# Pairwise bilinear products: two rows per partition, three large stores per row, three groups loaded ahead, later loads from the scalar queue

## The chip, the cores and the metric

One core of one Trainium2 chip. The metric is device microseconds of one execution, median of several. A single-core program's state is told from its own runs: fast when within 1.5% of the fastest of the same kernel. All runs compared here are fast; one experiment has a single timed run, whose state is unknown, and it is marked. A profile gives a span that is 1.7 to 2.7 us shorter than the time of the same execution.

## The reference

```python
# x: (4096, 32, 64) float32, W: (64, 64) float32
vid = jnp.einsum('bfd,de->bfe', x, W)
idx_i, idx_j = jnp.triu_indices(32, k=1)        # 496 pairs i < j
return x[:, idx_i, :] * vid[:, idx_j, :]        # (4096, 496, 64)
```

It reads 33.6 MB and writes 520.1 MB, so writing is the task.

## The kernel before

The batch is cut into 32 tiles of 128; I call the work of one tile a row, since each partition holds one batch row of it. TensorE transposes the row and multiplies it with W, ScalarE copies the results to `vid`, VectorE makes the 31 products (field i with all j > i), and SyncE stores them in nine pieces from six buffers. Loads share SyncE's queue with the stores.

```python
    CHUNK = 66
    AHEAD = 2
    xpool = ctx.enter_context(tc.tile_pool(name="x", bufs=AHEAD + 1))
    opool = ctx.enter_context(tc.tile_pool(name="out", bufs=6))
    def load(t):
        xt = xpool.tile([P, F, D], F32, tag="x", name=f"x_{t}")
        nc.sync.dma_start(out=xt, in_=x[t * P : (t + 1) * P])
        return xt
    # ... (weights, identity)
    for t in range(NT):
        if t + AHEAD < NT:
            loaded.append(load(t + AHEAD))
        xt = loaded[t]
        # ... (16 transposes, 31 matmuls, 8 copies: vid)
        for c, (fields, size) in enumerate(chunks):
            ot = opool.tile([P, CHUNK, D], F32, tag="o", name=f"o_{t}_{c}")
            # ... (one tensor_tensor per field)
            nc.sync.dma_start(
                out=out[t * P : (t + 1) * P, start : start + size, :],
                in_=ot[:, :size, :],
            )
            start += size
```

## Time and profile before

| | before |
|---|---|
| time, median of the first 3 runs | 1330.84 us (1329.06 to 1335.5) |
| span of the profile | 1326.4 us |
| DMA share and rate from 100 to 700 us | 1.01, 425 GB/s |
| VectorE busy | 1142.0 us, 86% |
| data packets per DMA engine | 2,560 |
| stores | 288, of 0.9 to 2.2 MB |

How to read it: with a DMA share of one nearly everywhere, ask two questions only. Where is the share under one? And how many nanoseconds does an engine need per byte while it is one? The prediction works both out, and shows the lines. A view that matters throughout is the table of stretches: each line gives a stretch, its length, the granted TensorE clock, the DMA share (the mean busy share of the 16 engines) and GB/s.

### The profile page before, as it was taken

The page shows a single profiled execution, that of the slowest core. Times are in us where ns is not written, and L with a number is a line of the kernel's source. Part 1 is how long each engine was busy: PE and PEld are TensorE (multiplying, and loading weights), DVE is VectorE, ACT ScalarE, POOL GpSimd, SP SyncE. Part 2 cuts the span into 40 slices and gives each one's busy share as a digit, 9 for nine tenths or more (in the row PEclk, how much of TensorE's full clock was granted, in tenths as well). Part 3 has the DMA queues.
Part 4 walks back from the last instruction along what each step waited for, and adds up shares of the span by engine and source line. Part 5 has one row for each costly group of instructions (what it writes and reads, how often), then busy time and mean ns, then how long its engine had stood idle before and what let it go on. Part 6 is the DMA issues. An engine that isn't in the chain of part 4 may idle for free.

```text
span 1326.4 us, 7305 instructions
## 1 busy us (share of the span) xinstructions
PE 255.1 (19%) x2496; PEld 242.2 (18%) x2496; DVE 1142.0 (86%) x992; ACT 139.4 (11%) x257; POOL 0.7 (0%) x6
## 2 busy tenths in 40 slices
PE   5012220133201222103321022220122211233000
PEld 5012220133201222103321022220122211233000
DVE  5999888888888888889888888888888888988893
ACT  3011101011000110101101011010111010110000
POOL 0000000000000000000000000000000000000000
PEclk9566665555656666555565566655666655655555
DMA  6999999999999999999999999999999999999996
GB/s 270 403 429 431 427 418 427 422 429 423 421 423 421 428 428 423 425 425 426 428 427 425 425 426 428 426 424 426 425 424 428 420 429 425 418 428 430 425 430 292
DMA packets 46277, 554.16 MB, mean 418 GB/s; under 512 B 5280, under 2 KB 5280, under 8 KB 9376
## 3 DMA queue, kind: packets, MB, share of 16 engines
q1 hardware_dynamic: 46080, 553.67, 98.9%
q8 instruction: 19, 0.31, 0.1%
q14 instruction: 18, 0.15, 0.0%
q10 hardware_dynamic: 160, 0.03, 0.0%
HBM read 33.59 MB, written 520.09 MB: 417 GB/s over the span
## 4 chain that ended last, share of the span: by engine, by line
DMA 75%; DVE 21%; issue 2%; PE 1%; DVEq 0%; ACT 0%
DMA out_dram<-o 75%; DVE o L117 21%; DMA x<-in_r_x_dram 0%; PE pv L97 0%; PE pt L85 0%; DVEq L117 0%; ACT vid L106 0%; DVEq L151 0%
## 5 line engine op out<-in xcount | busy, mean ns | idle before, releaser
L117 DVE TENSOR_TENSOR o<-x,vid 128x1984 f32<-128x1984 f32 (+30 forms) x992 | 1142.0, 1219 | 163.6 <-DMA out_dram<-o 149.1
L85 PE MATMUL pt<-ident,x 128*128 128x128 f32 x512 | 111.0, 406 | 967.9 <-DMA x<-in_r_x_dram 967.5
L85 PEld LDWEIGHTS pt<-ident,x 128*128 128x128 f32 x512 | 100.5, 219 | 971.9 <-issue 970.9
L86 ACT COPY xT<-pt 128x512 f32<-128x512 f32 x128 | 74.2, 589 | 702.2 <-PE pt L85 702.1
L97 PE MATMUL pv<-w,xT 64*128 64x64 f32 x1984 | 146.5, 308 | 0.0
L97 PEld LDWEIGHTS pv<-w,xT 64*128 64x128 f32 x1984 | 141.7, 222 | 8.7 <-issue 8.7
L106 ACT COPY vid<-pv 128x512 f32<-128x512 f32 (+1 forms) x128 | 64.2, 585 | 386.9 <-DVE o L117 382.6
L86 ACT ACT_TABLE_LOAD x1 | 1.3, 1283 | 2.0 <-issue 2.0
masks.py:199 POOL TENSOR_SCALAR_AFFINE_SELECT ident<-ident 128x128 f32<-128x128 f32 x1 | 0.3, 295 | 0.1
masks.py:197 POOL MEMSET ident<- 128x128 f32 x1 | 0.2, 205 | 0.3 <-POOLq L142 0.3
L142 POOL MEMSET const-bfloat16-1.0<- 128x1 bf16 x1 | 0.1, 102 | 0.0
L142 POOL MEMSET const-uint8-127<- 128x1 uint8 x1 | 0.1, 102 | 0.0
L142 POOL MEMSET const-float32-0.0<- 128x1 f32 x1 | 0.1, 99 | 0.2 <-issue 0.2
L142 POOL MEMSET const-float32-1.0<- 128x1 f32 x1 | 0.1, 99 | 0.0
## 6 DMA issues: line engine op xcount, KB each, us to landing
out_dram<-o SPq DMA_DIRECT2D x64, 1824.0 KB, 23.1
out_dram<-o SPq DMA_DIRECT2D x32, 2112.0 KB, 22.2
out_dram<-o SPq DMA_DIRECT2D x32, 2016.0 KB, 21.7
out_dram<-o SPq DMA_DIRECT2D x32, 1984.0 KB, 21.5
out_dram<-o SPq DMA_DIRECT2D x32, 1952.0 KB, 24.3
out_dram<-o SPq DMA_DIRECT2D x32, 1696.0 KB, 23.9
out_dram<-o SPq DMA_DIRECT2D x32, 1568.0 KB, 23.2
x<-in_r_x_dram SPq DMA_DIRECT2D x32, 1024.0 KB, 24.1
```

The source lines that it names most:

```text
L85: nc.tensor.transpose(pt[:, k, :], xt[:, f : f + 2, :], ident)
L86: nc.scalar.copy(xT[:, g * TPB : (g + 1) * TPB, :], pt)
L97: nc.tensor.matmul(pv[:, h, k, :], lhsT=xT[h * D : (h + 1) * D, pair, :], rhs=w2[h * D : (h + 1) * D, :], start=True, stop=True,)
L106: nc.scalar.copy(vid[:, g * GRP + k0 : (g + 1) * GRP, h, :], pv[:, h, k0:, :])
L117: nc.vector.tensor_tensor(ot[:, at : at + n, :], xt[:, i : i + 1, :].to_broadcast([P, n, D]), vid[:, i + 1 :, :], ALU.mult,)
L142: nc = _bacc.Bacc("TRN2", target_bir_lowering=False, num_devices=1)
```

## The change

The intent: fewer and longer packets, more work queued before the first store is ready, and loads that don't stand behind stores. The diff, cut to its core:

```diff
+SLOTS = [(0, 6), (6, 13), (13, 31)]
+FIRST = [(13, 31, [24, 18, 13]), (6, 13, [10, 8, 6]), (0, 6, [4, 2, 0])]
+SECOND = [(0, 6, [2, 4, 6]), (6, 13, [8, 10, 13]), (13, 31, [18, 31])]
-    AHEAD = 2
+    R = 2
+    G = B // (P * R)
+    SLOT = 171
+    AHEAD = 3
+    xg = x.rearrange("(g p r) f d -> g p r f d", p=P, r=R)
+    og = out.rearrange("(g p r) n d -> g p r n d", p=P, r=R)
-    opool = ctx.enter_context(tc.tile_pool(name="out", bufs=6))
+    opool = ctx.enter_context(tc.tile_pool(name="out", bufs=3))
+    def load(g):
+        queue = nc.sync if g < AHEAD else nc.scalar
+        xt = xpool.tile([P, R, F, D], F32, tag="x", name=f"x_{g}")
+        if g == 0:
+            h = F // 2
+            nc.sync.dma_start(out=xt[:, 0, h:, :], in_=xg[g][:, 0, h:, :])
+            nc.sync.dma_start(out=xt[:, 0, :h, :], in_=xg[g][:, 0, :h, :])
+            # ... (the second row as a third load)
+        else:
+            queue.dma_start(out=xt, in_=xg[g])
+    for g in range(G):
+        xt = loaded[g]
+        for r in range(R):
+            # ... (vid of this row, four fields at a time; row 0 from the last field down)
+            for s, (lo, hi) in enumerate(SLOTS):
+                # ... (rows 0 and 1 in the pieces of FIRST and SECOND, later rows whole)
+                ot = opool.tile([P, SLOT, D], F32, tag="o", name=f"o_{t}_{s}")
+                    nc.sync.dma_start(
+                        out=og[g][:, r, off[a] : off[b], :],
+                        in_=ot[:, off[a] - base : off[b] - base, :],
+                    )
+        if g + AHEAD < G:
+            loaded.append(load(g + AHEAD))
```

More of the change, by code (lines that the diff above doesn't have):

```diff
@@ L10 @@
 ALU = mybir.AluOpType
-def field_chunks(nf, most):
-    chunks, cur, size = [], [], 0
-    for i in range(nf - 1):
-        n = nf - 1 - i
-        if cur and size + n > most:
-            chunks.append((cur, size))
-            cur, size = [], 0
-        cur.append(i)
-        size += n
-    chunks.append((cur, size))
-    return chunks
+SLOTS = [(0, 6), (6, 13), (13, 31)]
+FIRST = [(13, 31, [24, 18, 13]), (6, 13, [10, 8, 6]), (0, 6, [4, 2, 0])]
+SECOND = [(0, 6, [2, 4, 6]), (6, 13, [8, 10, 13]), (13, 31, [18, 31])]
 @with_exitstack
@@ L37, in pairwise_bilinear_kernel @@
     B, F, D = x.shape
-    NT = B // P
+    NP = F * (F - 1) // 2
+    R = 2
+    G = B // (P * R)
     TPB = 4
-    GRP = 8
-    NGRP = F // (2 * GRP)
-    CHUNK = 66
-    AHEAD = 2
+    GRP = F // 2 // TPB
+    SLOT = 171
+    AHEAD = 3
+    xg = x.rearrange("(g p r) f d -> g p r f d", p=P, r=R)
+    og = out.rearrange("(g p r) n d -> g p r n d", p=P, r=R)
+    off = [i * (F - 1) - i * (i - 1) // 2 for i in range(F)]
     const = ctx.enter_context(tc.tile_pool(name="const", bufs=1))
-    xpool = ctx.enter_context(tc.tile_pool(name="x", bufs=AHEAD + 1))
-    tpool = ctx.enter_context(tc.tile_pool(name="xT", bufs=2))
+    xpool = ctx.enter_context(tc.tile_pool(name="x", bufs=AHEAD))
+    tpool = ctx.enter_context(tc.tile_pool(name="xT", bufs=1))
     vpool = ctx.enter_context(tc.tile_pool(name="vid", bufs=2))
-    opool = ctx.enter_context(tc.tile_pool(name="out", bufs=6))
+    opool = ctx.enter_context(tc.tile_pool(name="out", bufs=3))
     ps_t = ctx.enter_context(
-        tc.tile_pool(name="ps_t", bufs=3, space=bass.MemoryType.PSUM)
+        tc.tile_pool(name="ps_t", bufs=4, space=bass.MemoryType.PSUM)
     )
@@ L57, in pairwise_bilinear_kernel @@
     )
-    def load(t):
-        xt = xpool.tile([P, F, D], F32, tag="x", name=f"x_{t}")
-        nc.sync.dma_start(out=xt, in_=x[t * P : (t + 1) * P])
-        return xt
-    loaded = [load(t) for t in range(min(AHEAD, NT))]
     w2 = const.tile([P, D], F32)
@@ L69, in pairwise_bilinear_kernel, with project @@
     nc.scalar.dma_start(out=w2[D : 2 * D, :], in_=w)
+    def load(g):
[5 more added lines that the diff above has]
+            nc.sync.dma_start(out=xt[:, 0, :h, :], in_=xg[g][:, 0, :h, :])
+            for r in range(1, R):
+                nc.sync.dma_start(out=xt[:, r], in_=xg[g][:, r])
+        else:
+            queue.dma_start(out=xt, in_=xg[g])
+        return xt
+    loaded = [load(g) for g in range(AHEAD)]
     ident = const.tile([P, P], F32)
     make_identity(nc, ident)
-    chunks = field_chunks(F, CHUNK)
-    for t in range(NT):
-        if t + AHEAD < NT:
-            loaded.append(load(t + AHEAD))
-        xt = loaded[t]
-        xT = tpool.tile([P, F // 2, P], F32, tag="xT", name=f"xT_{t}")
-        for g in range(F // 2 // TPB):
-            pt = ps_t.tile([P, TPB, P], F32, tag="pt", name=f"pt_{t}_{g}")
-            for k in range(TPB):
-                f = 2 * (g * TPB + k)
-                nc.tensor.transpose(pt[:, k, :], xt[:, f : f + 2, :], ident)
-            nc.scalar.copy(xT[:, g * TPB : (g + 1) * TPB, :], pt)
-        vid = vpool.tile([P, F // 2, 2, D], F32, tag="vid", name=f"vid_{t}")
-        for g in range(NGRP):
-            pv = ps_v.tile([P, 2, GRP, D], F32, tag="pv", name=f"pv_{t}_{g}")
-            for k in range(GRP):
-                pair = g * GRP + k
+    def project(xt, r, tag, order):
+        xT = tpool.tile([P, F // 2, P], F32, tag="xT", name=f"xT_{tag}")
+        vid = vpool.tile([P, F // 2, 2, D], F32, tag="vid", name=f"vid_{tag}")
+        for g in order:
+            pairs = range(g * TPB, (g + 1) * TPB)
+            pt = ps_t.tile([P, TPB, P], F32, tag="pt", name=f"pt_{tag}_{g}")
+            for k, pair in enumerate(pairs):
+                nc.tensor.transpose(
+                    pt[:, k, :], xt[:, r, 2 * pair : 2 * pair + 2, :], ident
+                )
+            nc.scalar.copy(xT[:, g * TPB : (g + 1) * TPB, :], pt)
+            pv = ps_v.tile([P, 2, 2 * TPB, D], F32, tag="pv", name=f"pv_{tag}_{g}")
+            for k, pair in enumerate(pairs):
                 for h in range(2):
-                    if pair == 0 and h == 0:
-                        continue
                     nc.tensor.matmul(
@@ L103, in pairwise_bilinear_kernel @@
                     )
-            for h in range(2):
-                k0 = 1 if g == 0 and h == 0 else 0
-                nc.scalar.copy(
-                    vid[:, g * GRP + k0 : (g + 1) * GRP, h, :], pv[:, h, k0:, :]
-                )
-        vid = vid.rearrange("p g h e -> p (g h) e")
-        start = 0
-        for c, (fields, size) in enumerate(chunks):
-            ot = opool.tile([P, CHUNK, D], F32, tag="o", name=f"o_{t}_{c}")
-            at = 0
-            for i in fields:
-                n = F - 1 - i
-                nc.vector.tensor_tensor(
-                    ot[:, at : at + n, :],
-                    xt[:, i : i + 1, :].to_broadcast([P, n, D]),
-                    vid[:, i + 1 :, :],
-                    ALU.mult,
-                )
-                at += n
-            nc.sync.dma_start(
-                out=out[t * P : (t + 1) * P, start : start + size, :],
-                in_=ot[:, :size, :],
-            )
-            start += size
+            nc.scalar.copy(
+                vid[:, g * TPB : (g + 1) * TPB].rearrange("p k h e -> p h k e"),
+                pv[:, :, :TPB, :],
+            )
@@ new lines, in project, with products @@
+        return vid.rearrange("p g h e -> p (g h) e")
+    def products(xt, vid, ot, base, r, fields):
+        for i in fields:
+            n = F - 1 - i
+            nc.vector.tensor_tensor(
+                ot[:, off[i] - base : off[i] - base + n, :],
+                xt[:, r, i : i + 1, :].to_broadcast([P, n, D]),
+                vid[:, i + 1 :, :],
+                ALU.mult,
+            )
+    for g in range(G):
+        xt = loaded[g]
+        for r in range(R):
+            t = g * R + r
+            first = t == 0
+            vid = project(xt, r, t, range(GRP - 1, -1, -1) if first else range(GRP))
+            plan = FIRST if first else SECOND if t == 1 else None
+            for s, (lo, hi) in enumerate(SLOTS):
+                if plan:
+                    lo, hi, ends = plan[s]
+                else:
+                    ends = [hi]
+                ot = opool.tile([P, SLOT, D], F32, tag="o", name=f"o_{t}_{s}")
+                base = off[lo]
+                at = hi if first else lo
+                for e in ends:
+                    a, b = (e, at) if first else (at, e)
+                    products(xt, vid, ot, base, r, range(b - 1, a - 1, -1) if first else range(a, b))
+                    nc.sync.dma_start(
+                        out=og[g][:, r, off[a] : off[b], :],
+                        in_=ot[:, off[a] - base : off[b] - base, :],
+                    )
+                    at = e
+        if g + AHEAD < G:
+            loaded.append(load(g + AHEAD))
```

## The prediction

> **What bounds the kernel now.** I began with the page's slices and its DMA packets line, since a kernel that writes 520 MB is likely held by its transfers.
>
> ```profile
> DVE  5999888888888888889888888888888888988893
> DMA  6999999999999999999999999999999999999996
> GB/s 270 403 429 431 427 418 427 422 429 423 421 423 421 428 428 423 425 425 426 428 427 425 425 426 428 426 424 426 425 424 428 420 429 425 418 428 430 425 430 292
> DMA packets 46277, 554.16 MB, mean 418 GB/s; under 512 B 5280, under 2 KB 5280, under 8 KB 9376
> HBM read 33.59 MB, written 520.09 MB: 417 GB/s over the span
> ```
>
> The DMA engines are full in 38 of 40 slices at about 425 GB/s; only the first and last slices are low. VectorE is at eight or nine tenths, so it is next in line, but not the bound. The waits say the same.
>
> ```profile
> DVE o L117 <- DMA out_dram<-o: 149.1, 172, 2.3
> DVE o L117 <- ACT vid L106: 14.5, 1, 14.5
> ...
> SPq L124 <- DVE o L117: 1151.0, 288, 16.7
> SPq L151 <- DMA out_dram<-o: 19.3, 1, 19.3
> ```
>
> VectorE waits 149 us for stores to free its output buffers. The last store takes 19.3 us to land after everything else. SyncE's long wait is only an issuer waiting for its next job. Then the stretches, to see where the DMA engines are not full (the columns after each stretch's length are the granted TensorE clock, the DMA share and GB/s).
>
> ```profile
> 2.00:9.50 7.50, 1.00 0.95 395
> 9.50:19.50 10.00, 1.00 0.04 16
> 19.50:100.00 80.50, 0.59 1.01 417
> 100.00:700.00 600.00, 0.56 1.01 425
> 700.00:1312.00 612.00, 0.56 1.01 426
> 1312.00:1326.40 14.40, 0.50 0.28 119
> ```
>
> Two holes. From 9.5 to 19.5 us nothing moves: three loads are done, and the first store is issued only at 18.8 us, after transposes, matmuls, copies and two products. From 1312 us only some of the 16 engines still work. Between the holes a faster compute engine buys nothing; only fewer nanoseconds per byte would.
>
> **A model of the transfers.** The trace's packet records, grouped by size, give medians of 272 ns (7,168 B), 309 (8,192), 469 (12,544) and 629 (16,896). They lie on a line: 0.03677 ns per byte plus 8.4 ns per packet. Each engine also writes a 4-byte completion packet (9 ns) per transfer. One engine moves a sixteenth of 553.65 MB, 34.603 MB, in 2,560 data packets (32 loads and 288 stores of 8 each) and 320 completions: 1272.2 + 21.5 + 2.9 = 1296.6 us. To test it I subtracted this cumulative sum from the 16 landings of each transfer. The earliest landing of each keeps a constant distance (within 0.2 us) from about the 12th transfer to the 230th, nearly 1,000 us: the fastest engine runs exactly at the model with no idle time. The latest landing falls behind it by 0.4 us at first, 3 us after 160 us, 12 us after 550 and 14 or 15 from 900 on. The steps come mostly at the x loads (about 0.2 to 1 us each), and some at the 16 KB instruction fetches. So the span is 1296.6 + about 14 of start (latency plus hole) + 15 of the slowest engine's lag + 0.7 of end = 1326.3, against 1326.4 measured. The tail is this lag, not the size of the last store.
>
> [...]
>
> **The change, part by part.**
>
> *Packets.* Stores: three per row instead of nine, the first two rows in 9 and 8 pieces: 30 x 3 + 17 = 107 transfers. Loads: 15 of 16 KB per partition, plus group 0 in three pieces: 18. Each gives an engine 8 packets, 1,000 instead of 2,560, and 125 completions instead of 320. The store packets are 39 and 44 KB. If each stays one packet: 1272.2 + 8.4 + 1.1 = 1281.7 us, a gain of 14.9. It counts in full, for the engines have no idle time to hide it in.
>
> *Start.* Three groups, 6.3 MB, are now ahead of the stores: 14.8 us of transfers instead of 7.4, so they last to about 17 us. (No bytes are added; only moved into the hole.) Meanwhile group 0's first half row should land near 4.4 us, the weights near 6.7 as before. Eight matmuls (1 us at the present 3.9 for 31) and one copy (0.6) put the first product at about 8.5. Seven short products, by their means of 218 to 618 ns less overlap, take 2.5 us: first store issued at about 11, of 0.9 MB. The next follow near 16, 22 and 26 us with 2.1, 2.6 and 2.0 MB. At 425 GB/s the work queued reaches to 19, 24, 30 and 35 us, always past the next issue. The hole closes. What is left is latency: the first load now lands at 5.6 us, 2.5 of it data, so about 3.2. Gain about 10.9.
>
> *Three output buffers of 5.6 MB instead of six of 2.1.* When the slowest engine lands a store, VectorE needs 11 to 13 us to refill that buffer (sums of the product means), plus some 2 to start the store; the other two buffers hold 25 us of work. So the slowest engine never starves, though the fastest may be held once it is over about 10 us ahead. The slowest sets the end, so this costs nothing. VectorE does the same 992 products: 35.7 us per row against 40 of transfers.
>
> *TensorE, ScalarE.* 64 more matmuls and regrouped copies, on engines 19 and 11 per cent busy: nothing. A scalar queue that blocks on a load waits for the same product that frees its next vid buffer, a row ahead: nothing.
>
> *The lag.* Thirteen loads run amid stores instead of 29, each twice the bytes. In the bursts before, the first four or five packets of a load on an engine nearly all took 309 ns, and slow ones (400 to 1,400) came later. That suggests that [...]reading in bursts is what costs. Dealt between 1.6 us stores, this should be milder. I choose 10 us for the lag and fetches, instead of 15: an estimate.
>
> *Sum.* 1281.7 + 3.2 + 10 + 0.7 = 1295.6 us of span. The times before are 4.4 above the profile's span (1330.84 against 1326.4). So 1300 us, 2.3% less: 14.9 from packets, 10.9 from the start, 5 from the lag.
>
> **The rivals.** (a) *Long packets are split*, say in two: 2,000 packets, only half the packet gain, 1308 us. For it: nothing over 16,896 B is in the trace. Against: 7 to 17 KB are all single packets on one line. (b) *Interleaved reads stall.* The 16 KB instruction fetches, dealt between stores, took 880 to 970 ns where the line says 611. If each of the 104 load packets per engine lost 0.3 us, 31 us would eat the gain: about 1320 to 1325. Against: [...]8 KB fetches took 309. (c) *The tail of 14 us stays or grows* because only three buffers bind the engines: 1305. (d) *Only the holes counted* and the steady rate stays 425 GB/s because HBM sets it: 1319. Against: the constant distance of the fastest engine[...]. (e) *Better*: the lag nearly vanishes with the burst reads, 1293. (f) *VectorE becomes the bound* for want of buffers: its idle share falls from 12%, but 12 us of slack per buffer speak against it.
>
> **Range and chances.** The line for two per cent is 1304.2 us (1330.84 x 0.98), only 4 above my number: (a), (b), (c) and (d) end above it; the main sum and (e) below. I give 1288 to 1318 eight times in ten; faster by over 2% 0.62, within 2% 0.35, slower 0.03.
>
> **What would show it.** Right: about 18,000 packets, store packets of about 1,617 ns (44 KB), a rate of 429 to 431 GB/s in the middle, no gap between 9.5 and 19.5 us, first store near 11 us, VectorE's waits for stores shorter in number and longer each, and a last stretch with a low DMA share of 10 us or less. Wrong: twice the store packets (a); load packets near 900 ns and a middle rate at or under 425 (b, d); an equally long tail (c); stretches in the middle with a DMA share clearly under 1, with VectorE full (f).

## The result, and the profile after

1301.91 us, median of four runs (1301.52 to 1302.08), against 1330.28 of the kernel before in the same rounds (1329.06 to 1335.5). The ratio is 0.9762, 95% interval 0.9728 to 0.9795. (A ratio is the mean of one kernel's fast runs over the mean of the other's in the same rounds, so not quite the ratio of the medians.) The span is 1300.3 us, 26.1 less. The medians differ by 28.4: the profiled run of the kernel before was one of its faster ones (1326.4, where its runs of later rounds have spans of 1325.7 to 1335.9).

The page of the changed kernel, the lines that answer to those in the prediction:

```profile
DVE  6999979889798897988979899798987979999991
DMA  9999999999999999999999999999999999999997
GB/s 384 430 421 439 428 430 436 423 432 430 428 429 430 434 422 436 435 422 433 433 429 431 423 434 424 430 435 428 433 426 427 437 421 430 434 433 431 436 431 318
DMA packets 18193, 554.12 MB, mean 426 GB/s; under 512 B 2160, under 2 KB 2160, under 8 KB 2544
```

The first slice is full now; the last is still low. The 18,193 packets, 46,277 before, are what one packet per partition and transfer gives, with the completions: the 44 KB packets were not split. The stretches of the changed kernel:

```profile
2.00:9.50 7.50, 1.00 0.99 378
9.50:19.50 10.00, 1.00 0.98 399
19.50:100.00 80.50, 0.61 1.02 430
100.00:700.00 600.00, 0.53 1.00 430
700.00:1200.00 500.00, 0.53 1.00 429
...
1285.90:1300.30 14.40, 0.50 0.39 170
```

Read each against its line of before. The 10 us hole, 16 GB/s then, moves 399 GB/s. The middle went from 425 to 430, with the same full share: more bytes per busy nanosecond. The last 14.4 us hold 0.39 instead of 0.28 of the engines, so the tail has changed little. The waits:

```profile
DVE o L112 <- DMA out_dram<-o: 130.2, 71, 4.7
...
DVE o L112 <- ACT vid L103: 11.1, 1, 11.1
```

VectorE still waits for stores, less often and longer each time (71 times up to 4.7 us, instead of 172 times up to 2.3). It remains ahead of the DMA engines. The issues on SyncE's queue, with start and length of the stretch in which they were issued:

```profile
2.11 1.34 SPq L72 DMA_DIRECT2D x<-in_r_x_dram  x2
13.61 44.99 SPq L137 DMA_DIRECT2D out_dram<-o  x12
```

The first store leaves at 13.61 us; before, at 18.80. I had said 11. It did no harm: the DMA share is 0.98 over the whole former hole, since 6.3 MB of loads are queued in front.

**The time split up.** I use the line of the prediction (0.03677 ns per byte, unrounded 0.036765, 8.4 ns per packet, 9 ns per completion) for each kernel's own packets. "Start" is 100 us less the time that the bytes of the first 100 us would have taken at the kernel's own middle rate (from 100 to 1200 us). Both are counted from the packet records, with a packet that runs across a boundary shared out by its time. (The table of stretches books it wholly where it starts; with packets of 1.6 us that would make the start of the changed kernel 1.3 us too small and its rest as much too large.) "Rest" is what remains of the span; most of it is how far the last of the 16 engines fell behind.

| kernel | span | line | start | rest |
|---|---|---|---|---|
| before | 1326.4 | 1296.6 | 13.6 | 16.2 |
| after | 1300.3 | 1281.7 | 4.8 | 13.8 |
| difference | 26.1 | 14.9 | 8.8 | 2.4 |

The line rests on packet durations, and those held: in the changed kernel the 7,680 packets of 43,776 B have a median of 1,618 ns (the line says 1,618) and the 3,840 of 39,424 B one of 1,458 (line 1,458). The table is of one run of each kernel; to which term the other 2.3 us between the medians belong, it can't say. Whether these shares are causes is for the experiments.

### The profile page after: what moved, and what is told of

Read it like the earlier page. It is cut to its first block, busy times and chain, and to the rows that moved or that the text cites. A ratio compares the mean times of both kernels' runs of the same rounds, so it can differ in the third digit from the quotient of the medians.

```text
span 1300.3 us, 6845 instructions
## 1 busy us (share of the span) xinstructions
PE 336.3 (26%) x2560; PEld 315.8 (24%) x2560; DVE 1132.8 (87%) x992; ACT 136.4 (10%) x257; POOL 0.7 (0%) x6
## 2 busy tenths in 40 slices
DMA packets 18193, 554.12 MB, mean 426 GB/s; under 512 B 2160, under 2 KB 2160, under 8 KB 2544
## 3 DMA queue, kind: packets, MB, share of 16 engines
q1 hardware_dynamic: 16128, 526.39, 94.5%
## 4 chain that ended last, share of the span: by engine, by line
DMA 62%; DVE 35%; issue 1%; PE 0%; DVEq 0%; ACT 0%
DMA out_dram<-o 61%; DVE o L112 35%; DMA x<-in_r_x_dram 0%; PE pt L88 0%; PE pv L96 0%; DVEq L166 0%; DVEq L112 0%; ACT vid L103 0%
## 5 line engine op out<-in xcount | busy, mean ns | idle before, releaser
L112 DVE TENSOR_TENSOR o<-x,vid 128x64 f32<-128x64 f32 (+30 forms) x992 | 1132.8, 1219 | 141.3 <-DMA out_dram<-o 130.2
L96 PE MATMUL pv<-w,xT 64*128 64x64 f32 x2048 | 230.0, 413 | 862.0 <-ACT vid L103 827.8
L96 PEld LDWEIGHTS pv<-w,xT 64*128 64x128 f32 x2048 | 218.2, 320 | 878.6 <-ACT vid L103 837.7
L103 ACT COPY vid<-pv 128x512 f32<-128x512 f32 x128 | 72.1, 587 | 1060.2 <-DVE o L112 971.3
L88 PEld LDWEIGHTS pt<-ident,x 128*128 128x128 f32 x512 | 97.6, 212 | 9.0 <-issue 5.3
L91 ACT COPY xT<-pt 128x512 f32<-128x512 f32 x128 | 66.4, 610 | 5.7 <-PE pt L88 5.6
## 6 DMA issues: line engine op xcount, KB each, us to landing
out_dram<-o SPq DMA_DIRECT2D x30, 4928.0 KB, 28.4
x<-in_r_x_dram SPq DMA_DIRECT2D x2, 2048.0 KB, 14.4
```

Source lines behind the costliest of these rows:

```text
L88: nc.tensor.transpose(pt[:, k, :], xt[:, r, 2 * pair : 2 * pair + 2, :], ident)
L91: nc.scalar.copy(xT[:, g * TPB : (g + 1) * TPB, :], pt)
L96: nc.tensor.matmul(pv[:, h, k, :], lhsT=xT[h * D : (h + 1) * D, pair, :], rhs=w2[h * D : (h + 1) * D, :], start=True, stop=True,)
L103: nc.scalar.copy(vid[:, g * TPB : (g + 1) * TPB].rearrange("p k h e -> p h k e"), pv[:, :, :TPB, :],)
L112: nc.vector.tensor_tensor(ot[:, off[i] - base : off[i] - base + n, :], xt[:, r, i : i + 1, :].to_broadcast([P, n, D]), vid[:, i + 1 :, :], ...
```

## The experiments

Each is one edit to the kernel before or to the changed one. All give correct results except the two without later loads, which are wrong on purpose. All numbers of "rest" and "start" are worked out as above. The kernel before ran beside each of them; its runs scatter by 0.8 per cent (1327.5 to 1337.7 us), those of the changed kernel by 0.04% in its own rounds. The changed kernel did not run again beside its variants. A span is that of one run too, so a difference of two or three us from the kernel before is within its scatter.

### More loads ahead, alone

```diff
-    AHEAD = 2
+    AHEAD = 6
```

> The kernel before with six loads ahead of the first store instead of two or three; nothing else. Theory of the start: 6.3 MB of loads last to about 17 us, the first store still comes at 18.8, so the hole of 10 us shrinks to about 3: 1323 us, about 7 less, and the rate in the middle stays 425 GB/s. Rival (the hole is free, since those loads were hidden later anyway): 1330.

Measured: 1320.42 us (1316.28 to 1325.32), ratio to before 0.9919 (0.9895 to 0.9942); span 1319.1. Its stretches:

```profile
9.50:19.50 10.00, 1.00 1.01 422
19.50:100.00 80.50, 0.64 0.97 404
```

The first of the next stretches alone, and the issue of the first store:

```profile
19.50:25.00 5.50, 1.00 0.53 220
22.04 0.35 SPq L124 DMA_DIRECT2D out_dram<-o  x1
```

The hole has moved and shrunk to 2.6 us (what is missing from a full share in those 5.5 us). I had forgotten that the loop issues one more load before the first row's work, seven in all; they fill the time up to 19.5 us. But the first store leaves at 22.04 us instead of 18.80: the 31 matmuls of the first row (62 records) took 7.09 us while the loads ran beside them, 3.99 before, when nothing moved. Start falls from 13.6 to 7.0, rest (15.5) and middle rate (425 GB/s) stay. The gain is 7.3 us by the spans and 10.6 by the medians: the hole was on the path.

### Three stores per row, alone

```diff
-    opool = ctx.enter_context(tc.tile_pool(name="out", bufs=6))
+    opool = ctx.enter_context(tc.tile_pool(name="out", bufs=3))
+    slots = [range(0, 6), range(6, 13), range(13, 31)]
-        for c, (fields, size) in enumerate(chunks):
-            ot = opool.tile([P, CHUNK, D], F32, tag="o", name=f"o_{t}_{c}")
+        for c, fields in enumerate(slots):
+            ot = opool.tile([P, 171, D], F32, tag="o", name=f"o_{t}_{c}")
 # and the store after the last field of a slot; in row 0 also at the old piece ends
```

> The kernel before with three large stores per row from three 5.6 MB buffers from row 1 on (row 0 in ten pieces, so that the start is as before); loads, their queue and one row per partition as before. Theory of packets: 1,080 data packets and 135 completions per engine instead of 2,560 and 320, so 14 us less: 1316 us, middle rate 430 GB/s, hole at the start unchanged. Rival (HBM sets the rate): 1330 and 425 GB/s. Rival (three buffers starve the engines): over 1330.

Measured: 1315.31 us (1314.45 to 1316.23), ratio 0.9881 (0.986 to 0.9902); span 1312.7.

```profile
9.50:19.50 10.00, 1.00 0.12 48
19.50:100.00 80.50, 0.58 0.99 414
100.00:700.00 600.00, 0.57 1.00 430
700.00:1200.00 500.00, 0.55 1.00 431
```

The hole is as before, and the middle has the changed kernel's rate with loads in the old queue and one row per partition. The span fell by 13.7 (the medians by 15.7), the line said 14.1; start (14.8) and rest (15.4) are near those of before. The higher rate comes from fewer packets or from the larger buffers, which changed with them; the next run takes the two apart.

### Nine stores per row put back

```diff
+                cuts = {0: [2, 4, 6], 6: [8, 10, 13], 13: [17, 21, 31]}[lo]
-                    nc.sync.dma_start(
-                        out=og[g][:, r, off[a] : off[b], :],
-                        in_=ot[:, off[a] - base : off[b] - base, :],
-                    )
+                    for c in [e] if plan else cuts:
+                        # one store of fields at..c, from the same buffer
```

> The changed kernel with each large store issued as three at the same moment from the same buffer: 287 stores instead of 107. Buffers, loads, start and queues unchanged. Theory of packets: 2,440 data packets and 305 completions per engine instead of 1,000 and 125, 13.7 us more: 1315 to 1316 us, middle rate 425 GB/s. Rival (larger buffers or the second queue raised the rate): 1302.

Measured: 1310.34 us (1309.91 to 1310.74), ratio to before 0.9843 (0.9822 to 0.9863); span 1309.0.

```profile
19.50:100.00 80.50, 0.64 1.01 426
100.00:700.00 600.00, 0.53 1.01 426
700.00:1270.00 570.00, 0.53 1.01 426
```

The rate is back at 426 with the same buffers, queues and start, so those three don't make it: fewer packets do. (By the line of packet durations it is the packets and not the size of a transfer: stores of 0.9 to 2.2 MB ran at 425 GB/s, of 5.0 to 5.6 MB at 430. No run changed the one without the other.) But the time rose by only 8.4 of the 13.7 us expected (the span by 8.7). The line explains the rate; what is missing is 1.0 in the start (3.8 instead of 4.8) and 4.0 in the rest (9.8 instead of 13.8). The tail is shorter with small stores: in the last 15 us the DMA share is 0.98, 0.94 and 0.19 per 5 us, and the 16 engines' landings of the last store are 6.0 us apart instead of 10.4. So in this kernel long packets win 13.7 us and give 4 back at the end. In the kernel before they gave nothing back (rest 16.2, then 15.4). Only with short stores do the dealt-in loads bring the rest to about what the prediction put down for lag and end, 10.7; why long stores beside them keep it up, no run shows.

### The old start in the changed kernel

```diff
-    AHEAD = 3
+    AHEAD = 2
-            h = F // 2
+            h = 0                       # group 0's first row in one load
 # ... (the load of the second half is taken out)
-            vid = project(xt, r, t, range(GRP - 1, -1, -1) if first else range(GRP))
-            plan = FIRST if first else SECOND if t == 1 else None
+            vid = project(xt, r, t, range(GRP))
+            plan = SECOND if t <= 1 else None
 # ... (and the products of row 0 in forward order)
```

> The changed kernel with the start of before: row 0 loaded whole and worked in forward order, and two groups (4.2 MB) ahead instead of three. Theory of the start: loads end near 12 us, the first store is issued near 19, so a hole of 8 to 9 us comes back: 1310 to 1311 us, middle rate unchanged at 430 GB/s. Rival (the start is free): 1302.

Measured: 1312.13 us (1309.66 to 1314.28), ratio 0.9856 (0.9833 to 0.9879); span 1307.7.

```profile
9.50:19.50 10.00, 1.00 0.29 121
19.50:100.00 80.50, 0.57 1.00 419
```

A hole comes back, and 7.4 us of span (10.2 of the medians). Start rises from 4.8 to 12.0, the middle stays at 430. From both sides the start is worth 7 to 11 us. More loads ahead did most of it in the kernel before; how the new order of the first row and the third group share it here, this run does not say, for it undoes both.

### Later loads on the sync queue

```diff
-        queue = nc.sync if g < AHEAD else nc.scalar
+        queue = nc.sync
```

> The changed kernel with the later loads issued from the sync queue, behind the stores, as before. Theory ([...]only the order of packets changes): the same number of packets, middle rate 430 GB/s; loads come in bursts again, so the lag of the slowest engine is 10 to 14 us as in the run with three stores added to the kernel before: 1302 to 1306 us. Rival (the second queue is a source of the gain): 1310 or more and a lower middle rate.

Measured: 1303.4 us (1303.07 to 1303.62), ratio 0.9775 (0.9755 to 0.9795); span 1301.5, middle rate 431 GB/s. From the changed kernel's page, its loads and their us to landing (last column):

```profile
x<-in_r_x_dram ACTq DMA_DIRECT2D x13, 2048.0 KB, 23.0
```

And from this run's:

```profile
x<-in_r_x_dram SPq DMA_DIRECT2D x15, 2048.0 KB, 29.6
```

On the scalar queue a load lands in 23 us, behind the stores in 29.6; nobody was waiting for it two groups ahead (TensorE waits for the first load only, 5 us in both). The order of the packets does change: of the 1,664 later load packets 1,443 start just as a store's packet ends, on the sync queue 8, where 1,425 follow another load packet. But the two times differ by only 1.5 us of 1302, in different rounds, and the intervals of the ratios overlap almost wholly: a gain from the move is not shown. By queue the packets took 94.5% and 4.9% of the 16 engines' time in the changed kernel, and 99.2% on the sync queue alone here: about the same in all.

### One row per partition

```diff
-    R = 2
+    R = 1
-    AHEAD = 3
+    AHEAD = 6
```

> The changed kernel with one row per partition and six groups of 1 MB ahead, so the same bytes are loaded ahead and the stores are the same. Theory (packets alone): 16 more loads, 128 more packets per engine, 1.2 us more: 1303. The load packets dealt between the stores are 8 KB instead of 16 KB, so the lag may change by some us either way. Rival (two rows per partition matter for themselves, by the longer run in memory): 1310 or more and a lower middle rate.

Measured: 1300.77 us (1300.28 to 1302.06), ratio 0.9757 (0.9736 to 0.9777); span 1299.0, middle rate 430 to 431. Two rows per partition did nothing that shows; the line's 1.2 us are within what the rest varies by (11.8 here).

### Two output buffers

```diff
-    opool = ctx.enter_context(tc.tile_pool(name="out", bufs=3))
+    opool = ctx.enter_context(tc.tile_pool(name="out", bufs=2))
```

> The changed kernel with two output buffers instead of three. Theory of slack (11 to 13 us to refill, about 2 to start a store, against 13 us of work in the one other buffer): the engines now run dry between stores, so the DMA share in the middle falls clearly under 1 and the time rises to between 1340 and 1400. Rival (buffers have no part in it, VectorE at 87 per cent is ahead anyway): 1302.

Measured: 1406.52 us, one run, state unknown; span 1404.7.

```profile
100.00:700.00 600.00, 0.52 0.92 391
700.00:1200.00 500.00, 0.53 0.92 394
```

The DMA share falls to 0.92, and the time is a little above my range. One run is enough for 8 per cent. So the third buffer carries the change, and the slack reckoned for it in the prediction is real: with one other buffer, 13 us of work don't cover the 11 to 13 us of refill and the start of the store. With two buffers no engine could run ahead either: the 16 landings of the last store came within 0.2 us of each other (10.4 in the changed kernel).

### Where the lag of the slowest engine comes from

The prediction put the lag before down to loads, chose 10 us for the changed kernel, and expected dealt-in loads to be milder. So I took the loads away, in both kernels. First the changed one:

```diff
-            loaded.append(load(g + AHEAD))
+            loaded.append(loaded[g])
```

> The changed kernel without the thirteen later loads (the first three groups are used again; the result is wrong on purpose). Bytes and packets taken away are worth 63.6 us per engine by the line of 0.03677 ns per byte and 8.4 ns per packet. Theory (loads amid stores make the slowest engine lag): the last stretch shrinks to about 3 us, so 7 us more are gained: about 1231 us. Rival (the lag comes from instruction fetches[...]): lag still about 10 us, 1238.

Measured: 1237.42 us (1237.38 to 1237.47); span 1235.6. This is the rival's number, 1238: the theory falls for the changed kernel. (The cause that the rival names isn't shown by it.) The landings of the last store are still 10.4 us apart, with 15 engines within the first 1.8 us and one alone at the end. That one engine falls back by 0.4 us in most rows, nearly always at the middle store: about 100 of the 3,840 packets of 39,424 B take 50 to 80 ns over the line, several in sequence 1.5 us apart, as on one engine. Then the kernel before:

```diff
-            loaded.append(load(t + AHEAD))
+            loaded.append(load(t + AHEAD) if t == 0 else loaded[t - 1])
```

> The kernel before without the 29 later loads (the first three are used again; wrong result on purpose). Bytes and packets taken away: 72.1 us by the line. Theory (in the kernel before the lag of 12 us comes from the loads, where its steps were seen): the lag falls to about 3 us, so 81 us less: 1250. Rival (lag without loads too, as in the changed kernel): 1259.

Measured: 1249.0 us (1248.79 to 1249.3); span 1246.5. Here the theory holds: the last store's landings are 4.1 us apart instead of 12.2, and the rest falls from 16.2 to 9.9. The share in the run's last stretches shows a short tail:

```profile
1236.00:1241.00 5.00, 0.50 0.94 397
1241.00:1246.50 5.50, 0.50 0.21 90
```

So the loads made the lag in the kernel before, and in the changed kernel something at the middle store makes one just as large without them. As the end is set by the slowest single engine, two such causes on different engines need not add up, and taking one away may show little; that is my explanation, no run takes both away. Three more runs asked what the middle store has. First the place of the buffers in SBUF:

```diff
+    opool = ctx.enter_context(tc.tile_pool(name="out", bufs=3))
     const = ctx.enter_context(tc.tile_pool(name="const", bufs=1))
 # ... and removed further down
```

> The changed kernel with the output buffers allocated first, so that they lie elsewhere in SBUF; nothing else. In the run without later loads one engine still fell behind by 0.4 us per row, always at the middle store, and about 100 of its 3,840 packets of 39,424 B took 50 to 80 ns too long. Theory (it is the place of the second buffer in SBUF): those packets go, the lag shrinks from 10 to between 5 and 8 us: 1297 to 1300 us. Rival (it is the packet's size or its place in HBM, or what else runs at that moment): the group stays with the 39,424 B packets, 1302.

Measured: 1301.35 us (1300.72 to 1302.06), ratio 0.9767 (0.9742 to 0.9791). Theory wrong: the group stays (77 packets at 60 to 80 ns over the line, among those of 39,424 B; 7 among those of 43,776 B). Next, which buffer a slot gets:

```diff
+    spare = opool.tile([P, SLOT, D], F32, tag="o", name="o_spare")
+    nc.gpsimd.memset(spare[:, 0, 0:1], 0.0)
     for g in range(G):
```

> The changed kernel with one unused output tile taken first, so that the three slots of a row go to the second, third and first buffer. Theory (place of the second buffer): the group of about 100 packets that take 50 to 80 ns too long moves from the 39,424 B packets to the 43,776 B ones; time within 2 us of 1302. Rival (size, HBM place or moment): it stays with the 39,424 B packets.

Measured: 1301.17 us (1300.16 to 1303.02), ratio 0.9767 (0.9741 to 0.9793). Wrong again: 75 of the 39,424 B packets, 14 of the others. Last, the size:

```diff
-SLOTS = [(0, 6), (6, 13), (13, 31)]
+SLOTS = [(0, 6), (6, 14), (14, 31)]
-    SLOT = 171
+    SLOT = 172
```

> The changed kernel with the boundary between the second and third slot moved by one field: from row 2 on the middle store is 44,032 B per partition and the last 39,168 B, with the same number of packets. Theory (the slow group of packets belongs to the middle store's place in the row or to its moment): a group of about 100 packets 50 to 80 ns over the line appears among the 44,032 B packets, and the lag and the time stay: 1300 to 1303 us. Rival (it belongs to packets of about 39 KB): the group appears among the 39,168 B packets. Third possibility (it belongs to just this size or start): the group is gone, the lag falls and the time is 1294 to 1298.

Measured: 1302.3 us (1300.98 to 1303.65), ratio 0.9779 (0.9755 to 0.9802). The group has moved to the 44,032 B packets of the middle store (60 at 60 to 80 ns over the line, 5 among those of 39,168 B). So it is not the buffer, its place or the packet's size, but the middle store's place in the output row or what else happens at that moment. The kernel before with three stores has the same middle store and hardly any such packets (2 of 3,968 between 50 and 300 ns over), so its place in the row alone can't be the whole cause either.

The kept traces show what happens at that moment: TensorE works on a later row. In the run without later loads, TensorE is busy for the whole of the time of the packets 50 to 80 ns over the line, and for 0.29 of the time of the middle store's packets on the line. In the changed kernel the two shares are 0.95 and 0.37. It is the same where such packets lie in other stores: 0.78 against 0.21 among those of 43,776 B in the kernel before with three stores, 1.00 against 0.22 among those of 14,592 B in the kernel before. And the steps of 0.4 us end with the middle store that lands at 1136 us; TensorE's last matmul ends at 1138. The 20 instruction fetches, about 0.3 us over the line each, are too few for it. This is a coincidence in time: no run moves TensorE's work, so the cause stays open.

In the changed kernel itself the loads still count. Of its middle store's packets 240 are more than 80 ns over the line, 80 us in all on the 16 engines, and during 0.81 of their time a later load's packet is under way (0.04 for those on the line). The landings drift apart by 7 us in all in the 11 rows whose middle store meets at least 20 packets of a load, and by 1 in the other 19.

None of the ten with correct results beats the changed kernel clearly; three are 0.6 to 1.1 us lower by the medians, with ratios whose intervals overlap almost wholly.

## Why the prediction was right

- **Packets: right.** The line said 14.9 us. Three stores alone in the kernel before gave 13.7 of span; the middle rate went to 430 there and back to 426 when nine stores were put back. Rivals (a), split packets, and (d), a rate that HBM sets, are out: median 1,618 ns for a 44 KB packet, and 430 GB/s.
- **Start: right.** Predicted 10.9; the split gives 8.8, undoing it 7.4 of span. The first product and store came later than I worked out (11.15 and 13.61 us instead of 8.5 and 11), which the queued loads covered. I had taken the matmuls' pace from the kernel before, where nothing moved beside them (64 ns for each of 62 records); beside the loads the first 48 records took 112 ns each, and 14 transposes ran before the first of them.
- **Interleaved reads, rival (b): out in its size.** The 1,664 load packets on the scalar queue had a median of 611 ns, just the line. Yet the cost moved to the stores beside them: among the 39,424 B packets one in a hundred took 1,990 ns or more, and the 240 slow ones above lost 80 us, 5 per engine, not 31. The 16 KB instruction fetches again took 880 to 970 ns, so these were a misleading model for loads of the same size.
- **Three buffers: right.** The run with two shows that they are needed, and with three the DMA share stays at 1.00 in the middle, so rival (f) is out. VectorE's idle share before its products barely changed (163.6 to 141.3 us).
- **Lag: wrong step.** I put it at 10 us instead of 15, a gain of 5, for loads dealt in between stores. (That a second queue would deal them in was my assumption; the changed kernel's trace shows it for 1,443 of the 1,664 later load packets, which start just as a store's packet ends.) The rest fell by 2.4 us, the spread of the last landings by 1.9 (12.23 to 10.35). The loads did matter before: their packets lost 155 us there on the 16 engines together, against the 80 us of the stores beside them now (all packets after the first 60 us: 212 and 154 us over the line). So dealing them in was milder, but the end is set by the slowest engine, not by the sum; and without any loads a slow group of packets at the middle store, which I could not foresee, holds one engine back as much. Rival (c), a tail that stays, is nearest to what happened: 1305 predicted for it; that the buffers bind the engines, its reason, is not shown. Two readings behind this step were off as well. The lag of 15 us was 12.2 at the last store; about 2 more are what even the first engine lost against the model after the 230th transfer. And followed engine by engine (393 of 464 chains of eight load packets can be), 7 to 13% of the first four packets took over 330 ns and 21 to 40% of the last four, but of those over 1,000 ns 29 in 32 are among the first four: so slow packets do not simply come late in a burst, as I had read it.
- **The total came out closer than its terms.** The span was predicted at 1295.6 and measured at 1300.3, the gain being 2.1 us smaller than predicted at the start and 2.6 smaller in the lag. I added 4.4 us from span to time, taking a median of other runs over the profiled run's span; for the changed kernel the profiled run's time (1302.08) is only 1.8 above its span. The errors of 4.7 and 2.6 us partly cancelled, which is luck: 1300 against 1301.9. With the boundary for two per cent at 1304.2, the 0.62 for faster was about as firm as the terms allowed.

## What to carry to other kernels

When the DMA engines are full, fit packet durations against packet sizes: slope and intercept (0.03677 ns per byte and 8.4 ns per packet here) tell at once what fewer packets are worth, and multiplying it out predicted the middle of this kernel to about a microsecond. Look then for the stretches where the engines are not full, and fill the first with transfers that have to be made anyway (8.8 us of start here). The last engine to finish sets the time (the 16 landings of the last store were 12.2 us apart before and 10.4 after), so take the 16 landings of a transfer apart before you put a tail down to the size of the last store, and keep as many buffers as cover refill and start (three here; with two the DMA share fell from 1.00 to 0.92).
